# Two index tables and an inverse root moved ahead of the first token tiles in a gated mixture-of-experts kernel

## The chip, the cores and the metric

The kernel runs on one core of a Trainium2 chip. The metric is the time of one execution on the device in microseconds (us). Engines are named as in the profile: PE is TensorE (products), DVE is VectorE, ACT is ScalarE, POOL is GpSimd, SP is SyncE, which here only issues DMAs. "SPq" lines are DMA issues of SP's sequencer.

## What is computed

2048 tokens (4 x 512) of width 512 pass two gated residual blocks. The first sends each token through one of four experts, chosen by its token number; expert e is one 512x512 matrix of `ctx_2048`, used for all three of the expert's weights. The second is a dense three-layer network whose result is added, weighted by two gates per token, into rows 0 to 7 of the output only.

```
def expert(h, ids, W):                       # W: (4, 512, 512)
    e = min(clip(ids, 0, 24999) // 6250, 3)
    z = einsum('bsd,fd->bsf', h, W[e])
    return einsum('bsf,df->bsd', silu(z) * z, W[e])      # gate and up product are the same z

def ffn(h):
    p = softmax(h @ wr.T); r, i = top_k(p, 2); g = r / sum(r)
    y = silu(silu(h @ w1.T) @ w3.T) @ w2.T
    out = zeros; for k in 0, 1: out[i[:, k]] += g[:, k] * y   # only rows 0..7 are hit
    return out

x = x + tanh(g_xattn) * expert(layernorm(x), ids, ctx)
x = x + tanh(g_ffn) * ffn(layernorm(x))
```

## The kernel before

**Sorting.** The kernel sorts the tokens by expert on the chip. From the token numbers (`idt`) it forms one-hot columns, counts them with products on PE and gets each token's place in an order in which each expert has whole tiles of 128 and a rest rounded up to 32. Places are inverted by products with one-hot matrices; the result, `tok` in PSUM, says for each of 17 tiles of 128 rows (NP) which token stands in each row. 13 tiles (NF) belong to one expert each; 4 are cut into four pieces of 32 rows with an expert of their own, so there are 13 + 16 = 29 matrix uses (NU).

**Tables.** All are made by DVE from `tok` and from `cut`, the borders of the experts' stretches.
- `from_row` (L305): the token to fetch for each row of each tile.
- `which0` (L245): the row offset of the first tile's matrix, made early.
- `which` (`matrix_table`, L284 to L301: the three operations `later`, `stepped`, and a sum): the offsets of all 29 matrix uses. It is called for uses 0 and 1 at L306 and for the other 27 at L857.
- `to_row` and `first` (`row_tables`, L311 to L331, seven operations): where each row goes in the output, and where the pieces of the four cut tiles go in the second block's layout. Called at L862.

**Expert tiles.** A tile passes these steps; `order` (L389) gives their sequence, tiles 0, 1, 2, 3, 4, 5 first.
- `load` (L436): SP reads the offset from the table into a register and issues the 1 MB load of the matrix `m` (7 buffers). For tile 1, POOL first copies the offset to `which1` (L847), and SP reads it from there.
- `gather` (L393): POOL fetches the tile's 128 token rows with an indirect DMA (`x`, 5 buffers).
- `centre` (L403): statistics (L346, L348) and subtraction of the mean (L407) on DVE. The first tile has `first_in` (L418) instead, which also transposes in two halves.
- `scale` (L408): `inverse_roots` (L351), nine small dependent operations per tile on DVE (bit trick and two corrections); several tiles given together are interleaved.
- `turn_in` (L413): four transposes on PE (`tp_a`) and a copy on ACT.
- `up` (L467): eight product instructions on PE (`z`), silu on ACT (L472), a product on DVE (L473) that gives `g`.
- `turn_mid` (L476): transposes of `g` (`tp_g`) and a copy on ACT.
- `down` (L482): eight product instructions (`y`), then DVE adds the residual (L487) and POOL scatters the rows to the output (L488).
- `norms` and `turn_out`: the second block's normalization and transposes.

**Second block.** `load_w` issues the loads of its weights on SP: `w1` (1 MB) and `wr` early, `w3` and `w2` at L899. `sums_of_w1` reads `w1` in passes i = 5 to 8 of the main loop; `wr` is first used in `logits`. Its products fill PE between and after those of the expert tiles.

**Order.** The order is written by hand: every engine runs its instructions in the order of the program text, and semaphores hold back an instruction whose inputs are not there. So what stands at L842 to L876 decides who is ahead of whom on each engine's queue. There DVE has: statistics and halves of tile 0; statistics and centring of tile 1; the inverse roots of tiles 0 and 1 together; the 27-use table; the row tables; then `g` of tile 0 (inside `up`). SP has: matrix 0, matrix 1, the two gate values (128 x 4 bytes each), matrix 2, `w1`, `wr`, matrix 3. POOL has: gather 0, the copy of `which1`, gathers 1 to 4. PE has transposes of tile 0, three quarters of its `z`, transposes of tile 1, the last quarter of `z`, three quarters of tile 1's `z`, transposes of tile 0's `g`. Ahead of that, `busy(21)` (L303) keeps PE occupied with products whose result nobody reads.

`positions` is a pool of buffers for the sorting; it is closed once the row tables are made (L863), and `ffp`, the pool for the second block's sums, is opened after it.

Of the kernel before, what the change touches and what calls it, by code (L numbers as in the profile page):

```python
# [11 lines left out]
I32 = mybir.dt.int32  # L12
I16 = mybir.dt.int16
AF = mybir.ActivationFunctionType
ALU = mybir.AluOpType
AX = mybir.AxisListType
# [3 lines left out]
P = 128  # L20
# [5 lines left out]
def tile_gated_moe_ffn(  # L26
# [40 lines left out]
    nc = tc.nc  # L67
    NT, D = x.shape
    E = ctxT.shape[0] // D
# [33 lines left out]
    def ct_(shape, dtype, name):  # L103
        if name in on_the_way:
            return pos.tile(list(shape), dtype, tag=name, name=name)
        return const.tile(list(shape), dtype, tag=name, name=name)
# [4 lines left out]
    gates = ct_([P, 2], F32, "gates")  # L111

    def load_w(src, name):
        w = ct_([P, KC, src.shape[1]], F32, name)
        nc.sync.dma_start(w, src.rearrange("(k p) f -> p k f", p=P))
        return w
# [15 lines left out]
    whole = ct_([P, 2, E], I32, "whole")  # L132
    nc.vector.memset(whole[:, 0, :], -P)
    nc.vector.memset(whole[:, 1, :], -Q)
    cut = ct_([P, 2 * E + 1], F32, "cut")
# [5 lines left out]
    steps = ct_([P, 2 * E - 1], F32, "steps")  # L141
# [21 lines left out]
    NU = NF + (NP - NF) * G  # L163
    place0 = ct_([P, NU], F32, "place0")
# [33 lines left out]
    def busy(n):  # L198
        for _ in range(n):
            nc.tensor.matmul(idle, ones, ones.unsqueeze(1).to_broadcast([P, D // P, P]), start=True, stop=True)  # L200
# [42 lines left out]
    which0 = ct_([P, 1], I32, "which0")  # L243
# [36 lines left out]
    which = ct_([P, NU], I32, "which")  # L280
    later = ct_([P, 2 * E, NU], F32, "later")
    stepped = ct_([P, 2 * E - 1, NU], F32, "stepped")

    def matrix_table(n0, n1):  # L284
        n = n1 - n0
        nc.vector.tensor_tensor(
            later[:, :, n0:n1],
            place0[:, n0:n1].unsqueeze(1).to_broadcast([P, 2 * E, n]),
            cut[:, 1 : 2 * E + 1].unsqueeze(2).to_broadcast([P, 2 * E, n]),
            ALU.is_ge,  # L290
        )
        nc.vector.tensor_tensor(
            stepped[:, :, n0:n1],
            later[:, 0 : 2 * E - 1, n0:n1],
            steps.unsqueeze(2).to_broadcast([P, 2 * E - 1, n]),
            ALU.mult,
        )
        with nc.allow_low_precision("whole numbers below 4096"):
            nc.vector.tensor_reduce(
                which[:, n0:n1], stepped[:, :, n0:n1].rearrange("p e n -> p n e"), AX.X, ALU.add  # L300
            )  # L301

    busy(21)  # L303
    from_row = ct_([P, NP], I32, "from_row")
    nc.vector.tensor_scalar(from_row, tok, -1.0, 0.0, ALU.add, ALU.max)  # L305
    matrix_table(0, 2)  # L306

    first = ct_([P, NU - NF], I32, "first")
    to_row = ct_([P, NP], I32, "to_row")
# [34 lines left out]
    def moments(xt, name):  # L344
        st = small.tile([P, 6], F32, tag="st", name=f"st_{name}")
        nc.vector.bn_stats(st, xt)  # L346
        mv = small.tile([P, 2], F32, tag="mv", name=f"mv_{name}")
        nc.vector.bn_aggr(mv, st)  # L348
        return mv
# [32 lines left out]
    def transposed(h, name):  # L382

        tp = ps_tp.tile([P, KC * P], F32, tag="tp", name=f"tp_{name}")
        for k in range(KC):
            nc.tensor.transpose(tp[:, k * P : (k + 1) * P], h[:, k * P : (k + 1) * P], ident)  # L386
        return tp

    order = [0, 1, 2, 3, 4, 5, NF, 6, 7, 8, NF + 1, 9, 10, NF + 2, 11, 12, NF + 3]  # L389
# [3 lines left out]
    def gather(p):  # L393
        xt = xp.tile([P, D], F32, tag="x", name=f"x_{p}")
        nc.gpsimd.indirect_dma_start(  # L395
            out=xt,
            out_offset=None,
            in_=x,
            in_offset=bass.IndirectOffsetOnAxis(ap=from_row[:, p : p + 1], axis=0),
        )  # L400
        xs[p] = xt

    def centre(p):  # L403

        mvs[p] = moments(xs[p], f"a{p}")
        hs[p] = work.tile([P, D], F32, tag="h", bufs=4, name=f"h_a{p}")
        nc.vector.tensor_scalar(hs[p], xs[p], mvs[p][:, 0:1], None, ALU.subtract)  # L407

    def scale(*ps):
        for p, rs in zip(ps, inverse_roots([mvs.pop(p) for p in ps], [f"a{p}" for p in ps])):  # L410
            rss[p] = rs

    def turn_in(p):  # L413
        tp = transposed(hs.pop(p), f"a{p}")
        hTs[p] = work.tile([P, KC * P], F32, tag="hT", bufs=2, name=f"hT_{p}")
        nc.scalar.copy(hTs[p], tp)

    def first_in(p):  # L418

        st = small.tile([P, 6], F32, tag="st", name=f"st_a{p}")  # L420
        nc.vector.bn_stats(st, xs[p])
        mvs[p] = small.tile([P, 2], F32, tag="mv", name=f"mv_a{p}")
        nc.vector.bn_aggr(mvs[p], st)
        hTs[p] = work.tile([P, KC * P], F32, tag="hT", bufs=2, name=f"hT_{p}")
        n = D // 2
        for i in range(2):
            h = work.tile([P, n], F32, tag="h", bufs=4, name=f"h_a{p}_{i}")
            nc.vector.tensor_scalar(
                h, xs[p][:, i * n : (i + 1) * n], mvs[p][:, 0:1], None, ALU.subtract
            )  # L430
            tp = ps_tp.tile([P, n], F32, tag="tp", name=f"tp_a{p}_{i}")
            for k in range(n // P):
                nc.tensor.transpose(tp[:, k * P : (k + 1) * P], h[:, k * P : (k + 1) * P], ident)
            nc.scalar.copy(hTs[p][:, i * n : (i + 1) * n], tp)  # L434

    def load(p):  # L436

        n0, n = (p, 1) if p < NF else (NF + (p - NF) * G, G)
        mats[p] = []
        for i in range(n0, n0 + n):  # L440
            at = nc.values_load(
                early[i] if i in early else which[0:1, i : i + 1],
                engines=[SP],
                min_val=0,
                max_val=(E - 1) * D,
                skip_runtime_bounds_check_because="an expert's number, times D",
            )
            m = mp.tile([P, KC, D], F32, tag="m", name=f"m_{i}")
            nc.sync.dma_start(m, ctxT[bass.ds(at, D), :].rearrange("(k p) f -> p k f", p=P))
            mats[p].append(m)  # L450
# [16 lines left out]
    def up(p, inside=None):  # L467
        z = ps_mm.tile([P, D], F32, tag="mm", name=f"z_{p}")
        expert_product(z, hTs.pop(p), p, inside)
        g = work.tile([P, D], F32, tag="g", bufs=2, name=f"g_{p}")  # L470
        rs = rss.pop(p)
        nc.scalar.activation(g, z, AF.Silu, scale=rs)  # L472
        nc.vector.scalar_tensor_tensor(g, z, rs, g, ALU.mult, ALU.mult)  # L473
        gs[p] = g
# [359 lines left out]
    def step():  # L834
        if running:
            r = next(running[0], 0)
            if r == 0:
                running.pop(0)
            if r in (0, SHORT):
                step()  # L840

    early = {order[0]: which0[0:1, :]}  # L842
    load(order[0])
    gather(order[0])

    which1 = ct_([P, 1], I32, "which1")
    nc.gpsimd.tensor_copy(which1[0:1, :], which[0:1, order[1] : order[1] + 1])  # L847
    early[order[1]] = which1[0:1, :]
    for i in range(1, 5):
        gather(order[i])  # L850
    load(order[1])
    nc.sync.dma_start(gates[:, 0:1], g_xattn.to_broadcast([P, 1]))
    nc.sync.dma_start(gates[:, 1:2], g_ffn.to_broadcast([P, 1]))
    first_in(order[0])
    centre(order[1])
    scale(order[0], order[1])
    matrix_table(2, NU)  # L857
    load(order[2])
    w1 = load_w(w1T, "w1")
    wr = load_w(wrT, "wr")  # L860
    load(order[3])
    row_tables()  # L862
    positions.close()  # L863
    ffp = ctx.enter_context(tc.tile_pool(name="ffp", bufs=1))
    up(order[0], inside=lambda: turn_in(order[1]))
    centre(order[2])
    scale(order[2])
# [10 lines left out]
    for i in range(2, NP + 2):  # L878
        if i < NP:
            up(order[i])  # L880
        if i + 1 < NP:
            turn_in(order[i + 1])
        if i + 2 < NP:
            centre(order[i + 2])
        if i + 3 < NP:
            gather(order[i + 3])
            load(order[i + 3])
        if i <= NP:
            down(order[i - 1])
        turn_out(order[i - 2])  # L890
        if i <= NP:
            norms(order[i + 2] if i + 2 < NP else None, order[i - 1])
        step()
        if i > NP:
            step()
        if 5 <= i < 9:
            next(summing)
        if i == 7:
            w3 = load_w(w3T, "w3")  # L899
            w2 = load_w(w2T, "w2")  # L900
        if i < NP:
            turn_mid(order[i])
        for b in range(NB):
            if last[b] == i - 2:
                hT_sums[b] = sums_of_hT(b)
                running.append(ffn(b))
        if last[0] != i - 2:
            step()
# [53 lines left out]
```

## Time and profile before

| | us |
|---|---|
| median of 3 runs (278.0 to 278.48) | 278.3 |
| the profiled execution's own time | 278.8 |
| its span, first to last instruction | 277.1 |
| PE busy in the span | 267.2 (96%) |
| DVE busy | 147.3 (53%) |
| ACT busy | 69.2 (25%) |
| POOL busy | 39.1 (14%) |
| first gather issued on POOL | 9.14 |
| first tile's statistics on DVE | 12.58 |
| second tile's statistics on DVE | 16.61 |
| the 27-use table and the row tables on DVE | 19.87 to 22.51 |
| third matrix's load issued on SP | 21.68 |

A line of a timeline reads: start in us, duration in us, engine, line of the program, operation, output<-inputs (partitions x elements, type), number of instructions merged into the line, and in brackets how long the engine had been idle before it and what ended that wait. Ends of PE's products are modelled: a product of 512 columns is shown as 0.59 us long, though in an unbroken stream they follow each other every 0.43 us. The span begins with the first instruction.

### The profile page before, as it was taken

How to read it: one execution, taken by the hardware profiler on the slowest of the kernel's cores; microseconds unless marked ns; L12 is line 12 of the kernel's file. 1: busy time of each engine (PE TensorE's matmuls, PEld its weight loads, DVE VectorE, ACT ScalarE, POOL GpSimd, SP SyncE). 2: the span in 40 equal slices, each digit the busy share in tenths (PEclk: the TensorE clock that was granted, in tenths of full speed). 3: DMA queues.
4: the chain of work that ended last, by engine and by line, in shares of the span. 5: the costliest groups of instructions: out<-in, count | busy, mean ns of one | idle time of the engine just before them, and what ended most of it. 6: DMA issues, size and time to landing. Idle time of an engine off the chain costs nothing.

```text
span 277.1 us, 3564 instructions
## 1 busy us (share of the span) xinstructions
PE 267.2 (96%) x1173; PEld 125.2 (45%) x1173; DVE 147.3 (53%) x596; ACT 69.2 (25%) x134; POOL 39.1 (14%) x62
## 2 busy tenths in 40 slices
PE   5888999999999999999999999999999999999994
PEld 2443555553454445444344344534345444444362
DVE  6369877777977769927354392516352620711000
ACT  2022222322322322124133132312113233311120
POOL 5510122221222102311110010101010000000000
PEclk9999999999999999999999999999999999999999
DMA  0775999656759998498305085001000000000000
GB/s 1 231 260 202 383 391 392 237 195 222 222 181 392 393 392 323 139 384 275 145 10 180 2 289 200 38 0 40 1 11 2 0 0 1 0 0 2 0 0 2
DMA packets 20722, 42.54 MB, mean 154 GB/s; under 512 B 2143, under 2 KB 2207, under 8 KB 20704
## 3 DMA queue, kind: packets, MB, share of 16 engines
q1 hardware_dynamic: 17952, 33.66, 34.4%
q0 software_dynamic: 2720, 8.65, 8.7%
q8 instruction: 9, 0.15, 0.2%
q14 instruction: 9, 0.07, 0.1%
q10 hardware_dynamic: 32, 0.01, 0.0%
HBM read 38.10 MB, written 4.47 MB: 154 GB/s over the span
## 4 chain that ended last, share of the span: by engine, by line
PE 91%; DVE 4%; DMA 3%; issue 1%; POOL 0%; DVEq 0%
PE y L459 21%; PE v L736 20%; PE z L459 19%; PE X L628 10%; PE Y L628 5%; PE tp_f L386 3%; PE tp_g L386 3%; PE tp_a L386 3%; PE Z L628 2%; DMA x<-in_x_dram,from_row 2%; PE acc L748 1%; PE lg L705 1%; PE accT L764 1%; DMA idt<-in_ids_dram 1%; PE o L820 0%
## 5 line engine op out<-in xcount | busy, mean ns | idle before, releaser
L459 PE MATMUL z<-m,hT 128*32 128x512 f32 (+1 forms) x232 | 61.8, 595 | 0.2 <-ACT hT L434 0.2
L459 PE MATMUL y<-m,gT 128*32 128x512 f32 (+1 forms) x232 | 61.4, 594 | 0.0
L736 PE MATMUL v<-w,s 128*128 128x512 f32 (+1 forms) x136 | 57.3, 570 | 0.0
L736 PEld LDWEIGHTS v<-w,s 128*128 128x128 f32 x136 | 25.0, 190 | 27.2 <-issue 26.7
L459 PEld LDWEIGHTS z<-m,hT 128*32 128x32 f32 (+1 forms) x232 | 22.6, 146 | 29.4 <-issue 28.1
L459 PEld LDWEIGHTS y<-m,gT 128*32 128x32 f32 (+1 forms) x232 | 22.6, 146 | 27.8 <-issue 27.8
L488 POOL DMA_INDIRECT out_dram<-x,to_row x17 | 17.2, 1010 | 87.6 <-DVE x L487 85.4
L395 POOL DMA_INDIRECT x<-in_x_dram,from_row x17 | 16.8, 989 | 76.2 <-DVE h_a L407 36.1
L473 DVE SCALAR_TENSOR_TENSOR g<-z,rs_a,g 128x512 f32<-128x512 f32 x17 | 12.7, 749 | 25.7 <-ACT g L472 25.7
L472 ACT ACTIVATE g<-z,rs_a 128x512 f32<-128x512 f32 x17 | 11.7, 688 | 51.2 <-PE z L459 50.7
L487 DVE SCALAR_TENSOR_TENSOR x<-y,tg,x 128x512 f32<-128x512 f32 x17 | 12.7, 749 | 17.3 <-PE y L459 17.3
L744 ACT ACTIVATE s<-v 128x512 f32<-128x512 f32 (+1 forms) x17 | 9.7, 572 | 41.9 <-PE v L736 41.9
L521 ACT COPY hT<-tp_f 128x512 f32<-128x512 f32 x13 | 7.6, 586 | 43.5 <-PE tp_f L386 43.5
L346 DVE BATCH_NORM_STATS2 st_a<-x 128x6 f32<-128x512 f32 x16 | 11.0, 688 | 9.9 <-DMA x<-in_x_dram,from_row 9.9
L628 PE MATMUL X<-T,S 128*128 128x512 f32 x32 | 15.0, 592 | 0.0
L386 PEld LDWEIGHTS tp_f<-ident,h_f 128*128 128x128 f32 x68 | 8.2, 141 | 10.2 <-issue 10.2
L386 PEld LDWEIGHTS tp_a<-ident,h_a 128*128 128x128 f32 x64 | 7.6, 141 | 10.2 <-issue 9.6
L346 DVE BATCH_NORM_STATS2 st_f<-x 128x6 f32<-128x512 f32 x17 | 11.8, 695 | 0.6
L479 ACT COPY gT<-tp_g 128x512 f32<-128x512 f32 x17 | 10.0, 586 | 8.0 <-PE tp_g L386 8.0
L646 DVE TENSOR_TENSOR s<-X,c 128x512 f32<-128x512 f32 x4 | 2.8, 692 | 16.2 <-PE X L628 16.2
L386 PE MATMUL tp_g<-ident,g 128*128 128x128 f32 x68 | 10.2, 273 | 1.0 <-DVE g L473 1.0
L386 PEld LDWEIGHTS tp_g<-ident,g 128*128 128x128 f32 x68 | 8.2, 141 | 5.5 <-issue 5.2
(164 smaller groups left out, 273.4 us busy)
## 6 DMA issues: line engine op xcount, KB each, us to landing
m<-in_ctxT_dram SPq DMA_DIRECT2D x29, 1024.0 KB
w<-in_w1T_dram SPq DMA_DIRECT2D x1, 1024.0 KB
w<-in_w3T_dram SPq DMA_DIRECT2D x1, 1024.0 KB
w<-in_w2T_dram SPq DMA_DIRECT2D x1, 1024.0 KB
x<-in_x_dram,from_row POOLq DMA_INDIRECT x17, 6.1
out_dram<-x,to_row POOLq DMA_INDIRECT x17, 6.1
wr<-in_wrT_dram SPq DMA_DIRECT2D x1, 64.0 KB
x_first<-out_dram SPq DMA_DIRECT2D x4, 4.0 KB
```

The source lines that it names most:

```text
L346: nc.vector.bn_stats(st, xt)
L386: nc.tensor.transpose(tp[:, k * P : (k + 1) * P], h[:, k * P : (k + 1) * P], ident)
L395: nc.gpsimd.indirect_dma_start(out=xt, out_offset=None, in_=x, in_offset=bass.IndirectOffsetOnAxis(ap=from_row[:, p : p + 1], axis=0),)
L459: nc.tensor.matmul(out_ps[i * n : (i + 1) * n, :], lhs[:, k * P + i * n : k * P + (i + 1) * n], m[:, k, :], start=(k == 0), stop=(k == KC ...
L472: nc.scalar.activation(g, z, AF.Silu, scale=rs)
L473: nc.vector.scalar_tensor_tensor(g, z, rs, g, ALU.mult, ALU.mult)
L479: nc.scalar.copy(gT, tp)
L487: nc.vector.scalar_tensor_tensor(xt, y, tg[:, 0:1], xt, ALU.mult, ALU.add)
L488: nc.gpsimd.indirect_dma_start(out=out, out_offset=bass.IndirectOffsetOnAxis(ap=to_row[:, p : p + 1], axis=0), in_=xt, in_offset=None, bou ...
L628: nc.tensor.matmul(out_ps, a[:, k, c * P : (c + 1) * P], bb[:, k, :], start=start and k == 0, stop=k == 1, skip_group_check=True,)
L736: nc.tensor.matmul(v, s1[:, k, c_b + t * P : c_b + (t + 1) * P], w3[:, k, c0 : c0 + n], start=(k == 0), stop=(k == KC - 1),)
L744: nc.scalar.activation(s2, v, AF.Silu)
```

## The change

- DVE makes the whole `which` table (all 29 uses) directly after `from_row`, and the row tables directly after that, before anything that waits for the first tile. `matrix_table` is gone.
- The inverse root of tile 0 is taken alone, between `first_in` of tile 0 and `centre` of tile 1; that of tile 1 is taken alone after its `centre`.
- POOL copies the offsets to a new buffer `held`: that of tile 1 after the first gather, as before, and the 27 others after the fifth gather. SP reads all offsets but the first from `held`, so the loads of matrices 2 and up wait for that second copy.
- On SP the gate values are loaded after matrix 2 instead of after matrix 1; `w1` and `wr` are loaded in the first pass (i = 2) of the main loop, behind the matrix of tile 5, instead of between matrices 2 and 3.

```diff
-    def matrix_table(n0, n1):
...
     busy(21)
     from_row = ct_([P, NP], I32, "from_row")
     nc.vector.tensor_scalar(from_row, tok, -1.0, 0.0, ALU.add, ALU.max)
-    matrix_table(0, 2)
+    nc.vector.tensor_tensor(
+        later,
+        place0.unsqueeze(1).to_broadcast([P, 2 * E, NU]),
+        cut[:, 1 : 2 * E + 1].unsqueeze(2).to_broadcast([P, 2 * E, NU]),
+        ALU.is_ge,
+    )
+    nc.vector.tensor_tensor(
+        stepped,
+        later[:, 0 : 2 * E - 1],
+        steps.unsqueeze(2).to_broadcast([P, 2 * E - 1, NU]),
+        ALU.mult,
+    )
+    with nc.allow_low_precision("whole numbers below 4096"):
+        nc.vector.tensor_reduce(which, stepped.rearrange("p e n -> p n e"), AX.X, ALU.add)
...
             at = nc.values_load(
-                early[i] if i in early else which[0:1, i : i + 1],
+                look_up(i),
...
-    early = {order[0]: which0[0:1, :]}
-    load(order[0])
-    gather(order[0])
-
-    which1 = ct_([P, 1], I32, "which1")
-    nc.gpsimd.tensor_copy(which1[0:1, :], which[0:1, order[1] : order[1] + 1])
-    early[order[1]] = which1[0:1, :]
-    for i in range(1, 5):
-        gather(order[i])
-    load(order[1])
-    nc.sync.dma_start(gates[:, 0:1], g_xattn.to_broadcast([P, 1]))
-    nc.sync.dma_start(gates[:, 1:2], g_ffn.to_broadcast([P, 1]))
-    first_in(order[0])
-    centre(order[1])
-    scale(order[0], order[1])
-    matrix_table(2, NU)
-    load(order[2])
-    w1 = load_w(w1T, "w1")
-    wr = load_w(wrT, "wr")
-    load(order[3])
     row_tables()
     positions.close()
     ffp = ctx.enter_context(tc.tile_pool(name="ffp", bufs=1))
+    held = ct_([P, NU], I32, "held")
+
+    def look_up(i):
+        return which0[0:1, :] if i == order[0] else held[0:1, i : i + 1]
+
+    load(order[0])
+    gather(order[0])
+    one = slice(order[1], order[1] + 1)
+    nc.gpsimd.tensor_copy(held[0:1, one], which[0:1, one])
+    load(order[1])
+    for i in range(1, 5):
+        gather(order[i])
+    rest = slice(order[1] + 1, NU)
+    nc.gpsimd.tensor_copy(held[0:1, rest], which[0:1, rest])
+    first_in(order[0])
+    scale(order[0])
+    centre(order[1])
+    scale(order[1])
+    load(order[2])
+    nc.sync.dma_start(gates[:, 0:1], g_xattn.to_broadcast([P, 1]))
+    nc.sync.dma_start(gates[:, 1:2], g_ffn.to_broadcast([P, 1]))
+    load(order[3])
     up(order[0], inside=lambda: turn_in(order[1]))
...
         if 5 <= i < 9:
             next(summing)
+        if i == 2:
+            w1 = load_w(w1T, "w1")
+            wr = load_w(wrT, "wr")
```

More of the change, by code (lines that the diff above doesn't have):

```diff
@@ L282, in tile_gated_moe_ffn @@
     stepped = ct_([P, 2 * E - 1, NU], F32, "stepped")
-    def matrix_table(n0, n1):
[L285 to L301, printed above, removed]
     busy(21)
```

## The prediction

> **What bounds the kernel now.** I read the page first, then TensorE's timeline, then the timeline of all engines between the first gather and TensorE's last stall. In the page, part 2 holds the busy tenths in 40 slices of 6.9 us, and part 4 the share of each engine in the chain that ended last:
>
> ```profile
> PE   5888999999999999999999999999999999999994
> ...
> PEclk9999999999999999999999999999999999999999
> ...
> PE 91%; DVE 4%; DMA 3%; issue 1%; POOL 0%; DVEq 0%
> ```
>
> TensorE is full from the fifth slice to the last but one, at full clock, and it is 91% of the chain. A list of what TensorE waited for between 24 and 270 us is empty. So the only time to win lies ahead of 24 us, and a shift there goes through to the end undiminished. TensorE's timeline there:
>
> ```profile
> 14.89 2.84 PE L459 MATMUL z<-m,hT 128*128 128x512 f32 x6 [0.20 <-ACT hT L434]
> 18.19 0.63 PE L386 MATMUL tp_a<-ident,h_a 128*128 128x128 f32 x4 [0.45 <-DVE v_a L361]
> 18.65 3.68 PE L459 MATMUL z<-m,hT 128*128 128x512 f32 x8
> 23.32 0.63 PE L386 MATMUL tp_g<-ident,g 128*128 128x128 f32 x4 [0.99 <-DVE g L473]
> ...
> 25.12 3.60 PE L459 MATMUL y<-m,gT 128*128 128x512 f32 x8
> 28.56 0.60 PE L386 MATMUL tp_g<-ident,g 128*128 128x128 f32 x4
> ```
>
> The reader is to see two stalls: one before 18.19 (turn_in of tile 1) and one before 23.32 (turn_mid of tile 0). Their true size is not the printed idle time, since ends are modelled: in the last two lines 8 products start at 25.12 and the next transpose at 28.56, 3.44 later, 0.43 a product. The group from 18.65 has its last product at 18.65+3.68-0.59 = 21.74 (0.59 is one product's length), so the transpose could have started at 21.74+0.43 = **22.17**, and the second stall is 23.32-22.17 = **1.15 us**. In the same way the first is 18.19-(14.89+6x0.43) = 0.72 us. The timeline of all engines says what they wait for:
>
> ```profile
> 8.68 0.18 DVE L305 TENSOR_SCALAR from_row<-tok 128x17 int32<-128x17 f32 x1 [0.75 <-PE tok L276]
> ...
> 9.14 1.12 POOL L395 DMA_INDIRECT x<-in_x_dram,from_row  x1 [4.26 <-DVE stepped L292]
> ...
> 10.28 0.18 POOL L847 COPY which<-which 1x1 int32<-1x1 int32 x1
> 10.62 0.97 POOL L395 DMA_INDIRECT x<-in_x_dram,from_row  x1 [0.16 <-issue]
> ...
> 12.58 0.69 DVE L421 BATCH_NORM_STATS2 st_a<-x 128x6 f32<-128x512 f32 x1 [3.22 <-DMA x<-in_x_dram,from_row]
> ...
> 16.61 0.69 DVE L346 BATCH_NORM_STATS2 st_a<-x 128x6 f32<-128x512 f32 x1 [2.41 <-DMA x<-in_x_dram,from_row]
> ...
> 19.87 0.38 DVE L286 TENSOR_TENSOR later<-place,cut 128x216 f32<-128x216 f32 x1
> ...
> 21.68 0.39 SPq L449 DMA_DIRECT2D m<-in_ctxT_dram  x1
> ...
> 22.34 0.17 DVE L329 TENSOR_SCALAR first<-psum 128x16 int32<-128x16 f32 x1
> 22.43 0.74 DVE L473 SCALAR_TENSOR_TENSOR g<-z,rs_a,g 128x512 f32<-128x512 f32 x1
> ```
>
> DVE has idle holes of 3.22 and 2.41 us before tiles 0 and 1 land, and then does both tables from 19.87 to 22.51 in front of the product g of tile 0, for which TensorE waits. The third matrix's load sits behind the same table (21.68).
>
> **What the Trainium skill says.** "SBUF — State Buffer", Who interferes with whom: a VectorE instruction with two SBUF inputs contends with a GpSimd instruction that reads SBUF, and whoever starts first holds the port for the whole instruction; for descriptor generation it only infers freedom. The trace leans to freedom: the scatter from 38.75 keeps its 1.02 us beside two-input operations, and these keep 0.15 to 0.21. But the gather at 9.14 takes 1.12, and one at 112.13, started under a 1.2 us two-input operation, 1.17, where the others take 0.95 to 0.98. "DMA: Bandwidth & Descriptors", Queues, rings and completion order: each DMA engine goes round-robin between the queues it has work for, packet by packet. The trace agrees only in part: a gather issued at 37.47 beside a full SP queue moved nothing until 41.9 and landed after 6.1 us.
>
> **The change part by part.**
>
> Tables moved. They begin where matrix_table(0,2) begins now, 8.77. The three full operations follow each other as at 19.87, 20.28, 20.67 (end 21.18), so which ends at 8.77+1.31 = 10.08 instead of 9.36; pad starts 1.21 after the first (21.08-19.87), and the seven operations of row_tables take 22.51-21.08 = 1.43: end 8.77+1.21+1.43 = 11.41. Cover: tile 0 lands at 12.58, 1.17 us later. Without that cover they would cost their 2.6 us in full. from_row stays ahead, so the first gather keeps its 9.14.
>
> The copy to held. POOL's first copy waits for which: 10.08 plus the 0.28 from DVE to POOL (8.86 to 9.14) = 10.36 instead of 10.28. Gathers 1 to 4 and, on SP, matrix 1 are queued behind: **+0.08 us** on tile 1's landing. The first gather now starts beside two-input table operations; bounds 0 (the scatter) and +0.39 (held off until stepped ends at 9.53); a gain has no source. I take +0.07, half of the 0.15 by which 1.12 exceeds 0.97. The second copy, 27 elements, is not in the trace: between 0.18 (this copy) and 0.40 (POOL's iota of 272); behind the fifth gather, which ends at 15.34, nothing is queued on POOL until the scatter near 29, so 0 on the path.
>
> One inverse root taken alone. A single one takes 24.43 to 26.29 = 1.86 us, the pair 17.96 to 19.96 = 2.00: 1.72 us more DVE work. Tile 0's runs 14.20 to 16.06, in the hole before 16.61 (margin 0.55; uncovered it would cost up to 1.86). Tile 1's runs 18.04 to 19.90. Tile 0's silu now waits for z (19.08+0.59 = 19.67) rather than rs: about 19.75 instead of 19.93, 0.69 long; g follows at 20.50 and ends at 21.24, so the transpose is ready by 21.38, before 22.17: **-1.15 us**, and 0.79 to spare.
>
> What is late next. The transposes of tile 2 come 1.34 after tp_g (24.66-23.32), at 23.51. DVE begins its statistics behind g at about 21.16 and h takes 1.42 (23.09 to 24.51): 22.58. Then the lone root, and g of tile 1 at about 25.2 for a slot at 28.56-1.15 = 27.41. All fit.
>
> SP's queue. The copy ends about 15.6; the issue follows 0.49 later (10.46 to 10.95): matrix 2 at about 16.1 instead of 21.68, first used near 27.9. The two gate loads go behind it instead of behind matrix 1; tanh needs them only before the last DVE operation of tile 0 at 28.83-1.15 = 27.7. Their 256 tiny packets ran from 16.5 to 19, when the engines were 38% busy; now they run some 4 us later, with about 3 us to spare. Matrices 3, 4 and 5 follow at once, w1 and wr behind matrix 5. w1 is first read in the loop's fourth pass, over 30 us on; at 0.39 MB/us the five MB before and with it need 13 us. Nothing on the path; gathers 2 to 4 get a full SP queue beside them (rival below).
>
> Sum: -1.15+0.08+0.07 = **-1.0 us**. Against the profiled execution's own 278.8 (span 277.1 and 1.7 around it) that is 277.8; that execution stood 0.5 above the median, so against 278.3 it is **277.3**. TensorE's first stall (0.72) stays.
>
> **The rivals.** (B) Tile 1 lands earlier too, because the gate packets are gone: the first stall shrinks, at most to where z of tile 0 binds, 0.72 more: about 276.7. For: tile 1's last packets dribbled in over 15 to 16.5. Against: the gates stand behind matrix 1 in one queue; 286 small packets are counted after 16.5. (C) Tables and descriptor writing hold each other: a gather held to 9.53 leaves -0.68; stepped held until the gather ends at 10.26 puts which at about 11.16 and the copy at 11.44, +1.16, and all is given back. Between 277.6 and 278.3, middle 277.9. (D) Slower: **tile 2 starves behind matrices 2 and 3**. Now SP is idle from 17 to 22 and tiles 2 to 4 land alone (tile 2 8.4 us after 11.89, 20.3). If its queue gets nothing until both have passed, 17.2+2x2.7 (1 MB at 0.39 MB/us) = 22.6, plus 0.9 for the tile, it lands at 23.5; its transposes wait for anything past 23.51-0.14-1.42 = 21.95, and the gain is gone from 22.95 on: +0.55 net, 278.9. Against it: tile 2 is queued 3 us before matrix 2.
>
> **How the numbers follow.** Forecast (A, 277.0 to 277.6) 0.62, B 0.13, C 0.15, D 0.10. No change means within 0.2%, 0.56 us, about what a measurement of this kernel can tell. Faster: A, B and 0.05 of C, 0.80; same: 0.10 of C and 0.03 of D, 0.13; slower: 0.07. The range runs from B's 276.7 to C's end, 278.2; below and above are left 0.06 and 0.11.
>
> **What would show it.** After the change: no DVE table later than 12; tile 0's g near 20.5; tp_g following z with no idle near 22.3; the copy near 10.4; matrix 2's issue near 16. Tile 1's statistics later than 17.2 speak for C, tile 2's after 22 with a DMA wait for D, tile 1's before 16.3 for B. The forecast falls if TensorE shows a new wait after 24.

## The result and the profile after

| | before | after |
|---|---|---|
| median, 20 runs each | 278.15 us | 277.52 us |
| ratio, after to before | | 0.9977, 95% interval 0.9966 to 0.9988 |
| profiled execution, own time and span | 278.8, 277.1 | 277.53, 275.8 |

The change saves 0.64 us (0.23%), between 0.33 and 0.95. The forecast was 277.3, a saving of 1.0 from 278.3.

The page of the changed kernel: busy tenths of PE, and the chain that ended last by engine.

```profile
PE   5889999999999999999999999999999999999994
...
PE 94%; DVE 2%; DMA 2%; issue 1%; ACT 0%; DVEq 0%
```

PE is now full from the fourth slice on. Its timeline, in the same stretch as before:

```profile
14.57 0.63 PE L427 MATMUL tp_a<-ident,h_a 128*128 128x128 f32 x4 [1.19 <-DVE h_a L422]
15.44 2.84 PE L453 MATMUL z<-m,hT 128*128 128x512 f32 x6 [0.24 <-ACT hT L428]
18.12 0.60 PE L380 MATMUL tp_a<-ident,h_a 128*128 128x128 f32 x4
18.56 3.72 PE L453 MATMUL z<-m,hT 128*128 128x512 f32 x8
22.12 0.60 PE L380 MATMUL tp_g<-ident,g 128*128 128x128 f32 x4
...
23.85 3.60 PE L453 MATMUL y<-m,gT 128*128 128x512 f32 x8
```

The wait before the transposes of g is gone: 22.12 follows the z group without idle. y of tile 0 starts at 23.85 instead of 25.12, 1.27 earlier. From there to the end the two PE streams keep step (the first product of the last stage, `o`, begins 246.26 after that y in both), so all of the gain between these two executions is made ahead of 24 us. The timeline of all engines:

```profile
8.88 0.18 DVE L286 TENSOR_SCALAR from_row<-tok 128x17 int32<-128x17 f32 x1 [0.74 <-PE tok L276]
...
9.35 1.13 POOL L389 DMA_INDIRECT x<-in_x_dram,from_row  x1 [4.45 <-DVE from_row L286]
...
10.50 0.18 POOL L849 COPY held<-which 1x1 int32<-1x1 int32 x1
...
11.49 0.29 DVE L323 TENSOR_SCALAR first<-psum 128x16 int32<-128x16 f32 x1
...
12.89 0.69 DVE L415 BATCH_NORM_STATS2 st_a<-x 128x6 f32<-128x512 f32 x1 [1.11 <-DMA x<-in_x_dram,from_row]
...
16.37 0.69 DVE L340 BATCH_NORM_STATS2 st_a<-x 128x6 f32<-128x512 f32 x1
...
20.34 0.75 DVE L467 SCALAR_TENSOR_TENSOR g<-z,rs_a,g 128x512 f32<-128x512 f32 x1 [0.77 <-ACT g L466]
```

The whole front stands 0.2 later here (from_row 8.88 against 8.68), half of it since the token numbers landed 0.10 later (DVE's first operation on them starts at 2.58 against 2.48), the rest in the sorting behind them. The tables end at 11.78, with 1.11 us to spare before tile 0; g starts 2.1 us sooner than at 22.43. DVE comes to tile 1's statistics at 16.37 without a wait, directly behind tile 0's lone inverse root (14.61 to 16.46): tile 1 had landed at about 15.83, 5.0 us after the start of its gather. So that root did not fit into the hole with the margin of 0.55 that the prediction gave it; it held the statistics back by about half a microsecond, and further down it is seen why this cost nothing.

### The profile page after: what moved, and what is told of

It reads as the page before. It is cut to its first block, busy times and chain, and to the rows that moved or that the text cites. A ratio compares the mean times of both kernels' runs of the same rounds, so it can differ in the third digit from the quotient of the medians.

```text
span 275.8 us, 3562 instructions
## 1 busy us (share of the span) xinstructions
PE 266.6 (97%) x1173; PEld 125.4 (45%) x1173; DVE 148.7 (54%) x593; ACT 69.3 (25%) x134; POOL 39.3 (14%) x63
## 3 DMA queue, kind: packets, MB, share of 16 engines
q0 software_dynamic: 2720, 8.65, 8.3%
## 4 chain that ended last, share of the span: by engine, by line
PE 94%; DVE 2%; DMA 2%; issue 1%; ACT 0%; DVEq 0%
PE z L453 22%; PE y L453 21%; PE v L730 20%; PE X L622 10%; PE Y L622 5%; PE tp_f L380 3%; PE tp_a L380 3%; PE tp_g L380 3%; PE Z L622 2%; PE acc L742 1%; PE lg L699 1%; DMA x<-in_x_dram,from_row 1%; DMA idt<-in_ids_dram 1%; PE accT L758 1%; PE o L814 0%
## 5 line engine op out<-in xcount | busy, mean ns | idle before, releaser
L380 PE MATMUL tp_f<-ident,h_f 128*128 128x128 f32 x68 | 10.4, 276 | 0.0
```

## The experiments

One theory stood at the start: two stalls of PE went, the table stall (1.15) and most of the first one (0.72), the latter because the gate packets no longer stand behind matrix 1. Against it: only the table stall went. The stream from the first y to `o` takes 246.25 to 246.27 us in every profile but those of e4 (246.73, said there) and of e0, e1, e2 and e5 (247.39 to 247.98, said in the last section). So the start of that y is the measure to read, beside the ratio of the time to the kernel before on the same chip. A range in brackets is a 95% interval.

### The changed kernel again, and the gate loads moved alone

`e0_after` is the changed kernel.

> The changed kernel again, on the same chip as the three variants beside it, so that they can be set against it. Theory T (two stalls of PE went: the 1.15 us before the transposes of tile 0's g, because the tables are off DVE's path, and most of the 0.72 us before tile 1's transposes, because the 256 tiny gate packets no longer stand behind matrix 1): 0.5 to 1.0 us below the kernel before; tile 1 lands about 4.3 us after its gather's issue, as in the first profile. Rival R (only the table stall went, tile 1's early landing in that one profile was chance): tile 1 lands anywhere from 4.3 to 6 us.

`e1_gates_back` is the changed kernel with this edit:

```diff
     load(order[1])
+    nc.sync.dma_start(gates[:, 0:1], g_xattn.to_broadcast([P, 1]))
+    nc.sync.dma_start(gates[:, 1:2], g_ffn.to_broadcast([P, 1]))
     for i in range(1, 5):
...
     load(order[2])
-    nc.sync.dma_start(gates[:, 0:1], g_xattn.to_broadcast([P, 1]))
-    nc.sync.dma_start(gates[:, 1:2], g_ffn.to_broadcast([P, 1]))
```

> The changed kernel with only the two gate loads back in their old place on SP, behind matrix 1. T: tile 1 lands again about 6 us after its gather, near 16.6; PE's first stall is 0.5 to 0.7 us again, the second stays gone; 0.2 to 0.6 us slower than the changed kernel. R: no difference to the changed kernel (within 0.2 us); tile 1 lands as it does there.

`e2_gates_only` moves the same two lines in the kernel before, from behind `load(order[1])` to behind `load(order[2])`.

> The kernel before with only the two gate loads moved behind matrix 2; tables, inverse roots and all else as before. T: tile 1 lands near 15.1, PE's first stall shrinks to 0.0 to 0.3 us, the second stays near 1.15; 0.3 to 0.7 us faster than before. R: same as before within 0.2 us. A third case: the gate values come so late (they now follow matrix 2, issued near 22) that tanh holds up tile 0's last step; then slower.

`e5_gates_start` is the changed kernel with the two lines directly behind the allocation of `gates`, after the load of the token numbers.

> The changed kernel with the two gate loads right behind the load of the token numbers, at about 1.3 us, when no other DMA runs. T: the gate packets meet neither tile 1 nor matrices 2 and 3: the 21 to 26 us stretch carries 350 to 400 GB/s instead of 120 to 340, tanh waits for no DMA; but nothing on PE's path waits for these, so same time as the changed kernel within 0.2 us. If the 256 packets run past 6 us they hold up matrix 0 and tile 0: slower by up to 1 us.

Ratios to the kernel before: e0 0.9966 (0.9948 to 0.9984), e1 0.9977 (0.9960 to 0.9995), e2 0.9993 (0.9974 to 1.0011) and e5 0.9973 (0.9952 to 0.9994). These intervals are too wide to decide between the two expectations; the profiles decide. Tile 1's statistics in e0 and, with the gates back behind matrix 1, in e1:

```profile
16.28 0.69 DVE L340 BATCH_NORM_STATS2 st_a<-x 128x6 f32<-128x512 f32 x1 [0.33 <-DMA x<-in_x_dram,from_row]
```

```profile
15.91 0.69 DVE L340 BATCH_NORM_STATS2 st_a<-x 128x6 f32<-128x512 f32 x1
```

In e1 they start without waiting for the DMA, so tile 1 landed *sooner* than in the changed kernel beside it; with the gates gone from there it came at 16.43 in e5. In the kernel before, the statistics start at 15.89 with the gates moved (e2) and at 16.00 with the gates in their old place (e12, below). The late landing does not go with the gates' place. That half of the theory is wrong: the landing scatters from execution to execution.

The gate packets do cost something elsewhere. DMA share and GB/s are the last two columns, the changed kernel first, then e5:

```profile
22.00:23.00 1.00, 1.00 (x7) 0.64 (x6) 0.90 (x5) 0.24 (x1) 0.00 (x0) 1.00 0.38 121
23.00:24.00 1.00, 1.00 (x7) 0.71 (x6) 0.86 (x5) 0.72 (x2) 0.00 (x0) 1.00 0.41 146
```

```profile
22.00:23.00 1.00, 1.00 (x7) 0.76 (x6) 0.90 (x5) 0.37 (x1) 0.00 (x0) 1.00 1.02 389
23.00:24.00 1.00, 1.00 (x7) 0.64 (x6) 0.83 (x6) 0.72 (x2) 0.00 (x0) 1.00 1.04 406
```

With 1 KB of gate values in 256 packets behind matrix 2 the engines run at a third of their rate for these 2 us. The same dip is there in e0 (195 and 127 GB/s), and not in e1 (416 and 404). The last value lands at 26.4:

```profile
26.46 0.20 ACT L869 ACTIVATE tg<-gates 128x2 f32<-128x2 f32 x1 [1.68 <-DMA gates<-in_g_ffn_dram]
```

Nothing on PE's path waits for these transfers in the changed kernel, so e5 gains no time. The tanh is done at 26.66, 0.9 us ahead of the DVE step that needs it (27.56); in e0 it is 0.11 ahead (27.33, 27.44). In e2, where the gates follow the late matrix 2, the third case of its expectation came, though only on DVE:

```profile
28.77 0.75 DVE L487 SCALAR_TENSOR_TENSOR x<-y,tg,x 128x512 f32<-128x512 f32 x1 [1.15 <-ACT tg L871]
```

That is 4.38 behind y, 0.67 later than in the kernel before (3.71), and PE shows no wait for it.

### The tables' place: once more in front of g

`e8_repeat`: the changed kernel, with the table code in a function that is called a second time.

```diff
     load(order[3])
+    matrix_table()
+    row_tables()
     up(order[0], inside=lambda: turn_in(order[1]))
```

> The changed kernel with all ten operations of the two tables done a second time (same values into the same buffers) at their old place, between tile 1's inverse root and tile 0's g; loads and gathers stay early. Theory T (what the change won is DVE's 2.6 us of tables standing in front of g): g of tile 0 starts near 22.5, PE waits 1.0 to 1.3 us before the transposes of g, and the time is 1.0 to 1.3 us above the changed kernel's, that is, near the kernel before. Rival R (the win came from matrix 2 and the gathers' neighbours being issued earlier): PE has no such wait or makes it up, time as the changed kernel's.

Ratio 1.0004 (0.9987 to 1.0020): the gain is gone, with loads and gathers as early as in the changed kernel. Its PE and DVE lines:

```profile
18.54 3.83 PE L456 MATMUL z<-m,hT 128*128 128x512 f32 x8
23.03 0.63 PE L383 MATMUL tp_g<-ident,g 128*128 128x128 f32 x4 [0.67 <-DVE g L470]
```

```profile
22.05 0.18 DVE L326 TENSOR_SCALAR first<-psum 128x16 int32<-128x16 f32 x1
22.14 0.75 DVE L470 SCALAR_TENSOR_TENSOR g<-z,rs_a,g 128x512 f32<-128x512 f32 x1
```

The stall is 23.03-(18.54+3.83-0.59+0.43) = 0.82 here, not 1.0 to 1.3. The theory's core holds, its size does not. All other parts of the change, matrix 2 issued early and `w1` and `wr` late among them, are in e8 too, and leave no gain that can be measured. Without the repetition, e3 below stands at 0.9975 on the same chip.

### The lone inverse root undone

`e3_pair`:

```diff
-    scale(order[0])
     centre(order[1])
-    scale(order[1])
+    scale(order[0], order[1])
```

> The changed kernel with the inverse roots of tiles 0 and 1 taken together again, after tile 1's centring. T: the pair ends about 2.0 us after tile 1's centring, near 19.8; g of tile 0 is ready by 21.4 at the latest, ahead of PE's 22.0 to 22.2: same time as the changed kernel within 0.2 us. Tile 1's statistics no longer wait behind tile 0's lone root, so they may start up to 0.5 us sooner when tile 1 lands early. Rival (the lone root is needed for the gain): a wait of PE before the transposes of g, 0.3 us or more, slower.

Ratio 0.9975 (0.9962 to 0.9988), the changed kernel's. PE has no wait before the transposes of g, although tile 1 landed late there (statistics at 17.07 after a DMA wait):

```profile
19.11 3.68 PE L453 MATMUL z<-m,hT 128*128 128x512 f32 x8
22.63 0.60 PE L380 MATMUL tp_g<-ident,g 128*128 128x128 f32 x4
```

22.63 is 19.11+3.68-0.59+0.43, directly behind z. The lone root adds nothing that these runs can show; with the tables gone the pair is done in time.

### Matrix loads not held behind the gathers

`e4_direct` drops both copies, and SP reads `which`:

```diff
-        return which0[0:1, :] if i == order[0] else held[0:1, i : i + 1]
+        return which0[0:1, :] if i == order[0] else which[0:1, i : i + 1]
...
-    nc.gpsimd.tensor_copy(held[0:1, one], which[0:1, one])
...
-    nc.gpsimd.tensor_copy(held[0:1, rest], which[0:1, rest])
```

> The changed kernel without the two copies to held: SP reads every offset but the first from the table itself, so matrices 1, 2 and the gate loads are issued from about 10.5 on, ahead of and beside gathers 1 to 4; gathers 1 to 4 start 0.3 us sooner. Theory D (a gather beside a full SP queue gets little): tile 1 lands 2 to 6 us later, PE's first stall is 2 us or more, tile 2 is late too: 2 to 5 us slower than the changed kernel. Rival (the DMA engines share fairly): tile 1 lands within 1 us of its time, the time within 0.5 us.

Ratio 0.9999 (0.9985 to 1.0013): again nothing is left, for another reason. DVE and PE:

```profile
17.76 0.69 DVE L340 BATCH_NORM_STATS2 st_a<-x 128x6 f32<-128x512 f32 x1 [1.50 <-DMA x<-in_x_dram,from_row]
```

```profile
19.34 0.63 PE L380 MATMUL tp_a<-ident,h_a 128*128 128x128 f32 x4 [1.25 <-DVE v_a L355]
```

Tile 1's statistics start 1.2 to 1.9 us later than in the other kernels with early tables (15.9 to 16.6, but for 17.07 in e3 and the delayed e9), and the first stall is 19.34-(15.25+6x0.43) = 1.51. Tile 1 landed 7.1 us after the start of its gather; where the other profiles have this number, it is 5.0 to 6.5, but for 3.5 in e6 below. Neither side of the expectation: less than starving, more than fair sharing. The transposes of g follow z at once. So with tables early, the gain is kept only if the loads are held behind the gathers. Which of the two copies does it is not separated. The profile is of an execution 0.7 us above the median of its runs, and 0.47 of this lies elsewhere, in one z group near 95 us (4.12 instead of 3.65 in e3).

`e6_copy_late` puts gather 1 ahead of the first copy:

```diff
+    gather(order[1])
     one = slice(order[1], order[1] + 1)
     nc.gpsimd.tensor_copy(held[0:1, one], which[0:1, one])
     load(order[1])
-    for i in range(1, 5):
+    for i in range(2, 5):
```

> The changed kernel with the copy of tile 1's offset, and so the load of matrix 1, behind gather 1 instead of ahead of it: gather 1 starts 0.3 us sooner and its 256 KB run before matrix 1's first packets. If tile 1's landing scatters between 15.1 and 16.6 because matrix 1 stands beside it: it lands at 14 to 15, PE's first stall is 0.1 us, 0.1 to 0.5 us faster than the changed kernel. If matrix 1 comes too late for its first use (near 19.4): PE waits before z of tile 1, slower. If the landing doesn't hang on matrix 1: no difference.

Ratio 1.0001 (0.9980 to 1.0023). Its profile is of an execution of 283.08 us, 5 us above the median, and is read only for the event that follows.

```profile
18.22 1.02 PE L453 MATMUL z<-m,hT 128*128 128x512 f32 x2
21.95 5.46 PE L453 MATMUL z<-m,hT 128*128 128x512 f32 x6 [2.70 <-DMA m<-in_ctxT_dram]
```

Tile 1 no longer makes PE wait (first stall 0.1), but matrix 1, issued at 12.47 instead of near 11, does. After the 2.70 us of waiting the six products take 5.46 instead of 2.74, at a granted clock of 0.50 (22 to 28 us); the two together are the 5 us. The interval reaches down to 0.9980, so a loss against the changed kernel is not certain; that such a wait, in a milder form, stands behind the 0.7 us of the other runs is argued, not shown.

### The kernel before once more

`e12_before` is the kernel before, unchanged.

> The kernel before once more, for a second profile of it. Theory S (the first profile of before had tile 1 landing late, 16.6, in a scatter of 15.8 to 17.1 that has nothing to do with the change, and so stood above the median): tile 1 lands elsewhere in that scatter, PE's first stall is 0.1 to 1.2 us accordingly, and the second stall is 1.1 to 1.2 us again whatever the first. Ratio 1.000 within its interval. Rival: the second stall changes with the first.

Ratio 1.0003 (0.9990 to 1.0016). Its PE lines:

```profile
8.44 6.59 PE L200 MATMUL idle<-ones 128*128 128x512 bf16 x21
14.87 0.60 PE L433 MATMUL tp_a<-ident,h_a 128*128 128x128 f32 x4
15.71 2.84 PE L459 MATMUL z<-m,hT 128*128 128x512 f32 x6 [0.24 <-ACT hT L434]
...
18.83 3.68 PE L459 MATMUL z<-m,hT 128*128 128x512 f32 x8
22.71 0.63 PE L386 MATMUL tp_g<-ident,g 128*128 128x128 f32 x4 [0.20 <-DVE g L473]
...
24.51 3.60 PE L459 MATMUL y<-m,gT 128*128 128x512 f32 x8
```

The rival holds: the table stall is 22.71-(18.83+3.68-0.59+0.43) = 0.36 in this execution of the *same* kernel. Two things moved. The 21 idle products took 6.59 us here instead of 4.70 (the first ones 0.43 each, not 0.22), so that PE reached the transposes of tile 0 at 14.87 instead of 14.02; and tile 1's statistics started at 16.00 instead of 16.61. The later PE is, and the sooner tile 1, the less PE waits for g. This is the key to the size of the gain; the sum is below.

### The cover in front of tile 0

`e9_cover`:

```diff
-    row_tables()
+    for _ in range(3):
+        row_tables()
```

> The changed kernel with the seven row table operations done three times ahead of tile 0 (same values into the same buffers), 2.86 us more DVE work there. The cover named in the prediction is 1.17 us between the tables' end and tile 0's landing. T: the tables end near 14.2, tile 0's statistics start 1.6 to 1.8 us late, z of tile 0 as well; PE's first stall (0.1 to 0.9) disappears in it, so 1.0 to 1.7 us slower than the changed kernel. If the cover were longer than thought (tile 0 could wait): less.

Ratio 1.0040 (1.0024 to 1.0056), 1.7 us above the changed kernel's 0.9977. The tables end at 14.40, and tile 0's statistics follow without a DMA wait:

```profile
14.32 0.69 DVE L415 BATCH_NORM_STATS2 st_a<-x 128x6 f32<-128x512 f32 x1
```

That is 1.43 later than in the changed kernel, and y of tile 0 is at 25.05, 1.2 later. The cover is as long as the prediction said. The runs fall in two groups, ten near 278.6 and eleven near 280.2. The upper ones show a granted clock of 0.989 to 0.994, the lower ones, to which the profile belongs, 0.995 or more; so a part of the 1.7 us goes with the clock, for a reason that is not known. The lower group alone stands about 0.95 us above the changed kernel.

### Tile 0's subtraction beside the gather

`e10_tt`:

```diff
-            nc.vector.tensor_scalar(
-                h, xs[p][:, i * n : (i + 1) * n], mvs[p][:, 0:1], None, ALU.subtract
+            nc.vector.tensor_tensor(
+                h, xs[p][:, i * n : (i + 1) * n], mvs[p][:, 0:1].to_broadcast([P, n]), ALU.subtract
             )
```

> The changed kernel with the two half subtractions of tile 0's mean written as a tensor_tensor with the mean broadcast, in place of tensor_scalar. In the profiles so far the first half took 0.35 us when it began up to 0.42 us after the fourth gather's start on POOL, and 0.50 to 0.59 when it began 0.48 or more after it, ending each time 0.12 after the gather's end. Theory L (tensor_scalar here is held off by POOL's descriptor writing, and a tensor_tensor is not): the first half takes 0.33 to 0.40 us whatever its phase, the second too (0.41 before); PE's first transpose follows tile 0's statistics by 1.45 us in every case, and the time is 0 to 0.25 us below the changed kernel's. Rival (any DVE operation is held off, or the long case has another cause): first half 0.5 us or more when it begins 0.48 after the gather's start.

`e11_tt_pair` is e10 with the edit of e3.

> The same, and the inverse roots of tiles 0 and 1 taken together after tile 1's centring, as a version that may beat the changed kernel: tile 1's statistics wait for nothing but its landing. 0 to 0.4 us below the changed kernel; ratio to the kernel before 0.996 to 0.998. If the lone root matters: a wait of PE before the transposes of tile 0's g.

Ratios 0.9962 (0.9952 to 0.9973) and 0.9976 (0.9966 to 0.9986). The first half in the changed kernel, beside POOL's fourth gather, and in e10:

```profile
13.84 0.59 DVE L422 TENSOR_SCALAR h_a<-x,mv_a 128x256 f32<-128x256 f32 x1
```

```profile
13.36 0.95 POOL L389 DMA_INDIRECT x<-in_x_dram,from_row  x1 [0.31 <-issue]
```

```profile
13.74 0.42 DVE L422 TENSOR_TENSOR h_a<-x,mv_a 128x256 f32<-128x256 f32 x1
```

tensor_scalar ends at 14.43, 0.12 after the gather; e10's gather runs 13.16 to 14.11, the operation begins 0.58 into it, later than any that was held, and still takes 0.42. It shows no hold (its second half takes 0.42 as well), though it is slower than the 0.35 of an unheld tensor_scalar. e10 has the lowest ratio of all, but its interval touches the changed kernel's, and e11 with the same edit shows none of it: a version that surely beats the changed kernel was not found.

## Why the prediction was right, and which term was off

**The mechanism** stands as predicted. The tables fit in front of tile 0 (end 11.62 with the 0.2 of this execution's late front, measured 11.78; e9 shows what lies beyond the cover). g starts at 20.34 (20.50), the transposes of g at 22.12 with no wait (22.3), y at 23.85, the copy on POOL at 10.50 (10.4), matrix 2 is issued at 16.25 (16.1). No new wait of PE appears after 24. With the tables repeated at the old place (e8) the gain is gone again.

**The term that was off** is the first one of the sum, "-1.15 us", and with it the saving: 1.0 was forecast, 0.64 measured. That the time came within 0.22 of 277.3 all the same is in part luck: the 278.3 that the forecast started from stood 0.15 above the median of the 20 runs. The stall was read in one execution as if it belonged to the kernel. Two chains meet at the transposes of g: DVE's, which starts with tile 1's landing, and PE's, which starts with z of tile 0. All profiles but that of e6, sorted by where the tables are (us; the statistics of tile 1, the start of z of tile 0 and the start of y of tile 0):

| kernel | tile 1 | z | y | y - tile 1 | y - z |
|---|---|---|---|---|---|
| before | 16.61 | 14.89 | 25.12 | 8.51 | 10.23 |
| e2 | 15.89 | 14.83 | 24.39 | 8.50 | 9.56 |
| e12 | 16.00 | 15.71 | 24.51 | 8.51 | 8.80 |
| e8 | 16.34 | 15.42 | 24.84 | 8.50 | 9.42 |
| after | 16.37 | 15.44 | 23.85 | 7.48 | 8.41 |
| e0 | 16.28 | 14.91 | 23.73 | 7.45 | 8.82 |
| e1 | 15.91 | 15.55 | 23.92 | 8.01 | 8.37 |
| e5 | 16.43 | 15.08 | 23.73 | 7.30 | 8.65 |
| e3 | 17.07 | 15.20 | 24.36 | 7.29 | 9.16 |
| e4 | 17.76 | 15.25 | 25.06 | 7.30 | 9.81 |
| e10 | 16.37 | 15.19 | 23.66 | 7.29 | 8.47 |
| e11 | 16.56 | 15.37 | 23.86 | 7.30 | 8.49 |
| e9 | 17.61 | 16.68 | 25.05 | 7.44 | 8.37 |

With tables in front of g, y comes 8.50 after tile 1, with z of tile 0 anywhere from 14.83 to 15.71. With tables early it comes at the later of tile 1 + 7.29 and z + 8.37 (to 0.2); the 7.29 is the way over tile 1's own transposes, that is, over the first stall. In the first profile after, z binds (23.81 against 23.66), which is why the half microsecond that the lone root cost tile 1's statistics was free. So the gain of an execution is about the smaller of 8.50-7.29 = 1.21 and tile 1 - z + 0.13. For the first profile that is 1.21, for e2 1.19, for e12 0.42: a mean of 0.94 over the three, against the 1.15 of the prediction. Tile 0 may take from it: its statistics follow the first gather by 3.40 to 3.53 in the three profiles without early tables, and 3.42 to 3.64 in the ten with them (e9 aside), and the held half of its subtraction costs up to 0.24. That these make up the rest to the measured 0.64 is argued: one profile for each kernel gives no distribution, and 0.94 is a mean over three.

**The smaller terms.** The copy's +0.08 did not come: the copy does not wait for `which`, which ends at 10.34, but follows the gather in both kernels (1.14 and 1.15 after its start), so it cost 0.01. The +0.07 for descriptor writing did not come where it was put: the first gather took 1.13 with tables beside it and 1.12 without. "TensorE's first stall (0.72) stays" was also one execution's number: it is 0.1 to 0.9 in the table's executions, but for e4. And "about 3 us to spare" for the gates was 0.9, and 0.1 to 2.0 in other executions with the gates in the same place (e0, e11).

**The rivals.** B's effect was seen (first stall 0.10 in the first profile after), its cause was not the gates (e1): against the first profile before, z of tile 0 began 0.55 later and tile 1's statistics 0.24 sooner. C, tables and descriptors holding each other, did not occur at the gathers; a hold did occur at tile 0's subtraction, which the prediction had not listed, and it is there in e12 as well (0.59), so it is not the change's. D did not occur: tile 2 never made DVE wait in the changed kernel. The half of D's premise that loads ahead of a gather delay it was shown by e4, for tile 1.

## What to carry to other kernels

A stall read in one profile is the difference of two chains, and each chain has its own scatter; before a stall is booked as a gain, name the first event of both chains, and book the smaller of the stall and what the other chain allows. Work without a deadline belongs in a hole that ends with a landing, and the hole's length against the work says what it costs. Where loads are freed from a wait, ask which transfer on the path they now run beside: here that was worth the whole gain (e4).

## What the hardware showed unexpectedly

- A DVE tensor_scalar from SBUF to SBUF in fp32 can be held by POOL's writing of gather descriptors. Begun up to 0.42 us after the gather's start it took 0.35; begun 0.47 to 0.57 after it, 0.50 to 0.59, with the end each time about 0.12 after the gather's (five profiles against six; in the six the second half, begun later, ends 0.11 to 0.13 after the gather too). The Trainium skill, "SBUF — State Buffer", Who interferes with whom, says that tensor_scalar can use the port pair shared with GpSimd and that the later one blocks until the first is done; the traces agree, with the refinement that an operation begun in the gather's first 0.42 us was not held. A tensor_tensor in its place took 0.42 (e10, e11); the same section infers that such an operation does not meet descriptor writing, as it uses only the pair's read side.
- Idle products meant to keep PE going ran at half rate for the first 3 to 4 us in e1, e9 and e12 (21 in 6.3 to 6.6 us instead of 4.7), with a granted clock of 1.00 printed throughout. They then *delay* the work behind them: in e12 the first half of tile 0 was ready for PE at 14.31 (13.58+0.59, and the 0.14 that PE follows by in the first profile after), and its transposes began at 14.87. What decides it no run here shows.
- On the chip of e0, e1, e2 and e5 the first block of router products (`lg`) took 1.1 to 1.7 us longer than in all other profiles, with nothing waited for that the profile shows. This is most of why times there stand about 1.5 us higher (median of the kernel before 279.93, against 278.22 and 278.36 on two other chips).
